# Graph and mixture-of-experts layers on one core: groups of two tiles in the second pass, and an expert's second products two steps behind its first

## The chip, the cores and the metric

The kernel runs on one core of a Trainium2 chip. The metric is the device time of one execution in microseconds (us): 2432.77 us, the median of three runs from 2429.38 to 2436.04. The profiled execution took 2431.52 us with a span of 2429.8 us; 1.7 us lie outside the span.

## The reference, cut to what matters

3125 nodes of 256 numbers pass two layers. Each layer adds a sum over a graph (103,125 edges) and an attention, then a mixture of eight experts. The change touches the second layer alone:

```
xn = layernorm(x)
agg = segment_sum((xn @ W[type])[src, type], dst)          # gathered rows, summed by target node
h = gelu(agg + xn @ loop_w + h_bias + xn)
x = x + layernorm(h) * ln_gamma + ln_beta + attention(xn)
xn = layernorm(x) * gamma + beta
w = softmax over the two largest of xn @ Wr + br           # 0 for the six other experts
for e in range(8):
    y = y + w[e] * (gelu(xn @ W1[e] + b1[e]) @ W2[e] + b2[e])   # W1 256x512, W2 512x256
x = x + y
```

All eight experts are computed for every node, in 32-bit floats.

## The kernel before, in words

The nodes are sorted by their number of edges and stand in 25 tiles of 128; tile 24 has 53 of them. `x` stays in SBUF for the whole kernel. The first layer writes a table of rows to HBM (`htab_f`); the second layer is the "second pass" of this text.

**Gathers.** The row sum of tile t takes STEPS[t] gathers (45 for tile 0 down to 22 for tile 24). Each is an indirect DMA that GpSimd (POOL) issues, and fetches one row of 256 numbers for each of the 128 nodes (L195). `edge_pass` (L1336) does the tiles in the order of GROUPS1 (L69). It takes up to four gathers at a time into a buffer `gt` (a *chunk*, L1358), and adds the chunk up on VectorE (DVE) with L1376 and a last addition L1378. The pool of `gt` has five buffers (L2013), so the gathers of a chunk can't start before the chunk five before it has been added. The tiles 1 to 4 (PAIRS) are gathered before that, in `first_groups` (L2572, additions in L2590).

**Groups.** When all tiles of a group are summed, its jobs go into a list (`after1`, L2544, `Group`, L2312). First come ten jobs that lead to the routing: `sums_a` to `sums_c` (the products with `loop_w`, L2326 to L2328, added by L2333, and a Gelu), `states_a` to `states_d` (two layer norms, with square roots on ScalarE (ACT), L2353), `routes_a` (transposes L2396 and the routing products L2404, both in a PSUM tile `pt`), `routes_b` (the two largest, L206 to L223 and L2417) and `shares` (the constants of the experts, L2456 and L2481). Then come ten steps (`step`, L2492). Step i takes what the step before left in PSUM (`take`, L2489 on DVE), issues the first products of expert i (`hidden`, L2436 on TensorE (PE), with a Gelu on ACT, L2441, into a buffer `hT1`), and the second products of expert i-1 (`outputs`, L2470) into one of two PSUM banks (`bank`, L2445). The last four steps of a group are put between the first jobs of the next group (`late`, L2542). Below, h3 stands for the `hidden` of expert 3, o3 for its `outputs`, and "loops" for the products L2326 to L2328.

**The order of the work.** After each chunk, `edge_pass` runs jobs worth a credit (L1383 to L1391): what the list costs divided by the gathers left in the group, kept between 0.9 and 1.3, for each gather. A job's cost is the number beside it in `jobs` (L2502). The order on DVE and POOL is exactly this program order (`manual_schedule`, L2601); PE's, ACT's and SP's order is the scheduler's. So a `take` stands on DVE between the additions of two chunks, and whatever it waits for, the next chunk's additions wait for too. The results of all tiles leave at the end, by scatters on POOL (L242).

Before the change the groups are, in order: tiles (3,4), (1,2), (23,24), (19 to 22), (15 to 18), (12 to 14), (9 to 11), (7,8), 6, 5 and 0.

Of the kernel before, what the change touches and what calls it, by code (L numbers as in the profile page):

```python
# [12 lines left out]
F32 = mybir.dt.float32  # L13
# [8 lines left out]
P = 128  # L22
# [11 lines left out]
NX = 8  # L34
F = 512
FC = F // P
# [27 lines left out]

MADE = tuple(range(1, 25)) + (0,)

CUTS1 = (25, 23, 19, 15, 12, 9, 7, 6, 5)
PAIRS = ((3, 4), (1, 2))
GROUPS1 = tuple(range(a, b + 1) for a, b in PAIRS) + tuple(range(b, a) for a, b in zip(CUTS1, CUTS1[1:])) + (range(0, 1),)  # L69

# [32 lines left out]
def gps_kernel(ctx: ExitStack, tc: tile.TileContext, a, out):  # L103
# [1216 lines left out]
    def fast():  # L1320
# [197 lines left out]
        def hidden(ts):  # L1518
            n, at0 = len(ts) * P, ts[0] * P
            for i in range(2):  # L1520
                if i not in hTs:
                    hTs[i] = f0h.tile([P, FC, 3 * P], F32, name=f"hT0_{i}", bufs=1)
                hT = hTs[i]
                for f in range(FC):
                    ph = ps_mm.tile([P, 512], F32, name="mm")
                    for c in range(2):
                        PE.matmul(  # L1527
                            ph[:, :n], w1[:, i, c, f * P : (f + 1) * P], xT[:, c, at0 : at0 + n],
                            start=(c == 0), stop=(c == 1),
                        )  # L1530
                    S.activation(hT[:, f, :n], ph[:, :n], AF.Gelu, bias=b1[:, i, f : f + 1])
# [57 lines left out]
        with ExitStack() as l0x:  # L1589
# [257 lines left out]
            class Fin0:  # L1847
# [46 lines left out]
                def jobs(self):  # L1894
                    def step(i):
                        if i < self.k:
                            self.products(i)
                        if i > 0:
                            self.sums(i - 1)

                    out = [(5.0 if 0 < i < self.k else 2.5, lambda i=i: step(i)) for i in range(self.k + 1)]
                    return out + [(2.0 * self.k, self.norms)]
# [21 lines left out]
            def after0(g, tiles, accs):  # L1924
                last = g == len(GROUPS) - 1
                if last:
                    fin[0].accs = accs
                    return
                bg.extend(Fin0(tiles, accs).jobs())
                if g == SURE:  # L1930
                    bg.extend(staged(guess(), (4.0, 3.0, 3.0, 2.0, 2.0, 2.0)))
                    for r in range(NX):
                        bg.extend(staged(relation(r), (1.5, 1.5)))
                for ts in GROUPS[: g + 1] if g == SURE else [tiles] if g > SURE else []:
                    bg.append((5.0 * len(ts), lambda ts=ts: hidden(ts)))
                    if waiting:
                        bg.append(waiting.pop())
                    bg.append((4.0 * len(ts), lambda ts=ts: (outputs_a(ts), outputs_out(ts))))
                    waiting.append((1.0 * len(ts), lambda ts=ts: outputs_b(ts)))
                if g == len(GROUPS) - 2:  # L1940
                    bg.append((4.0, lambda: None))
                    bg.append(waiting.pop())
                if g == len(GROUPS) - 2:
                    fin.append(Fin0(GROUPS[-1], None))
                    bg.append((2.5, lambda: fin[0].products(0)))
# [34 lines left out]
        with tc.If(again > 0):  # L1980
            w_full, rank = settled
            pick = f0k.tile([P, 2, NX], F32, name="pick")
            for i in range(2):
                V.tensor_scalar(pick[:, i, :], rank[:, 0, :], float(i), None, op0=ALU.is_equal)
            load_pair(pick)
            tmp = f0k.tile([P, NX], F32, name="tmp_c")
            V.tensor_tensor(tmp, w_full[:, 0, :], pick[:, 0, :], op=ALU.mult)
            V.reduce_sum(w_first, tmp, axis=AX.X)
            for ts in GROUPS:
                k = len(ts)  # L1990
                mv = small.tile([P, 4, 2], F32, name="mv1")
                rs = small.tile([P, 4], F32, name="rs1")
                for j, t in enumerate(ts):
                    V.tensor_tensor(x[:, t, :], x[:, t, :], bet, op=ALU.subtract)
                    stats(x[:, t, :], mv[:, j, :])
                rstd(mv[:, :k, :], rs[:, :k])
                for j, t in enumerate(ts):
                    normalize(xt_tok[:, t, :], x[:, t, :], mv[:, j, :], rs[:, j : j + 1])
                    V.tensor_tensor(x[:, t, :], x[:, t, :], bet, op=ALU.add)
                    to_xT(t, xt_tok[:, t, :])  # L2000
                if ts == GROUPS[-1]:
                    for i in range(2):
                        hidden_gelus(i, hidden_products(ts, i, phs[i]))
                else:
                    hidden(ts)
                    outputs_a(ts)
                    outputs_out(ts)
                    outputs_b(ts)
# [176 lines left out]
        with ExitStack() as l1x:  # L2185
# [20 lines left out]
            wf = l1w.tile([P, NT, NX], F32, name="wf")  # L2206

            fin = l1x.enter_context(tc.tile_pool(name="fin1", bufs=1))
            f1 = l1x.enter_context(tc.tile_pool(name="f1", bufs=3))
            wp = l1x.enter_context(tc.tile_pool(name="wp", bufs=1))  # L2210
            w1s, w2s = [None] * NX, [None] * NX

# [99 lines left out]
            class Group:  # L2312
# [114 lines left out]

                def hidden(self, e):
                    n, at0 = self.n, self.at0
                    hT = self.hT[e] = f1.tile([P, FC, 4 * P], F32, name="hT1")  # L2430
                    fs, w = max(4 // self.k, 1), self.k * P
                    for f0 in range(0, FC, fs):
                        ph = ps_mm.tile([P, 512], F32, name="mm")
                        for f in range(f0, min(f0 + fs, FC)):
                            for c in range(2):
                                PE.matmul(  # L2436
                                    ph[:, (f - f0) * w : (f - f0) * w + n], w1s[e][:, c, f * P : (f + 1) * P],
                                    xT[:, c, at0 : at0 + n], start=(c == 0), stop=(c == 1),
                                )
                        for f in range(f0, min(f0 + fs, FC)):  # L2440
                            S.activation(  # L2441
                                hT[:, f, :n], ph[:, (f - f0) * w : (f - f0) * w + n], AF.Gelu, bias=b1[:, e, f : f + 1]
                            )
# [48 lines left out]
                def step(self, i):  # L2492

                    self.take()
                    if i < NX:
                        self.hidden(i)
                    if 1 <= i <= NX:
                        self.outputs(i - 1)
                    if i == NX + 1:
                        leaving.extend(self.tiles)  # L2500

                def jobs(self):  # L2502
                    k = self.k
                    first = [
                        (2.0, self.sums_a), (2.0, self.sums_b), (1.0, self.sums_c), (1.0, self.states_a),
                        (1.0, self.states_b), (1.0, self.states_c), (1.0, self.states_d), (4.0, self.routes_a),
                        (2.0, self.routes_b), (2.0, self.shares),
                    ]
                    cost = [1.6] + [3.1] * (NX - 1) + [1.6, 0.5]
                    rest = [(c * k, lambda i=i: self.step(i)) for i, c in enumerate(cost)]  # L2510
                    return first, rest

# [100 lines left out]
    with tc.If(unfit < 1):  # L2613
        fast()
# [78 lines left out]
```

## Time and profile before

| what | us |
|---|---|
| median of three runs | 2432.77 |
| profiled execution | 2431.52 |
| its span | 2429.8 |
| second pass: its first gather ends | 1493 |
| last gather of the second pass starts | 2344.28 |
| last gelu jobs (tile 0, L2333) start | 2377.86 |
| last `take` starts | 2420.36 |
| last scatter starts | 2421.12 |

The page gives for each engine its busy time in the span, in 40 slices, and by groups of instructions. POOL's part in the second pass is an almost unbroken line of gathers: each is shown as busy for about 0.95 us, with 0.30 us of issue before it. The timeline gives every instruction with its start, its length, and in brackets how long its engine sat idle before it and for what. Adjoining instructions of one kind are merged into one row (x16). "PEclk" is the clock that PE was granted, as a share of full speed.

### The profile page before, as it was taken

Reading aid. Unit: us, or ns where it says so; the run is one execution under the profiler, and the core shown is the slowest. Engines: PE = TensorE matmul, PEld = TensorE weight load, DVE = VectorE, ACT = ScalarE, POOL = GpSimd, SP = SyncE. Lnnn points to the kernel's source line nnn. Section 1 sums busy time; section 2 is a strip of 40 time slices with the busy share of each in tenths; the row PEclk is TensorE's granted clock in tenths of the full one; section 3 lists DMA queues with packets and bytes.
Section 4 is the critical chain, followed back from the end, with each engine's and each line's share of the span. In section 5 each row is a group of like instructions: output and inputs, shape, how many; then the busy total and the mean of one; then the engine's idle time right before and its main releaser. Section 6 shows DMA issues by size and latency. Waiting matters only on the chain.

```text
span 2429.8 us, 20895 instructions
## 1 busy us (share of the span) xinstructions
PE 1689.2 (70%) x6033; PEld 1106.3 (46%) x6033; DVE 1236.6 (51%) x3393; ACT 532.4 (22%) x1263; POOL 1705.9 (70%) x1847
## 2 busy tenths in 40 slices
PE   3446697502946526267699836988687899989997
PEld 2323344301624313145344324766354566667786
DVE  7655555525534434344567435554543636465542
ACT  4313231001201101012222222322211222132343
POOL 4577777777777777777126777677777777777771
PEclk9777887855978667687799977998798999999999
DMA  6544434344444344444156754333333333333330
GB/s 197 146 109 110 110 105 129 105 108 137 108 107 107 105 109 106 108 105 107 58 186 240 268 166 149 94 104 103 108 101 110 104 104 110 107 103 103 102 101 19
DMA packets 124809, 289.03 MB, mean 119 GB/s; under 512 B 41258, under 2 KB 62830, under 8 KB 121480
## 3 DMA queue, kind: packets, MB, share of 16 engines
q0 software_dynamic: 83184, 230.02, 34.3%
q1 hardware_dynamic: 36970, 54.83, 6.7%
q10 hardware_dynamic: 4526, 2.71, 0.4%
q8 instruction: 51, 0.84, 0.1%
q14 instruction: 78, 0.64, 0.1%
HBM read 248.54 MB, written 38.89 MB: 118 GB/s over the span
## 4 chain that ended last, share of the span: by engine, by line
PE 23%; POOL 9%; issue 8%; DVE 5%; DMA 4%; ACT 1%; DVEq 0%; POOLq 0%; ACTq 0%
POOL gt L195 8%; PE mm L2436 7%; PE py L2470 7%; PE mm L190 7%; DMA gt<-htab_f,idx2g 3%; DVE gt L1376 1%; POOL out_dram L242 1%; DVE bnst L164 1%; PE pt L2404 1%; PE mm L2328 1%; PE mm L2326 0%; DVE x L2369 0%; DVE acc L1378 0%; DVE x L2489 0%; DVE hh L2368 0%
## 5 line engine op out<-in xcount | busy, mean ns | idle before, releaser
L195 POOL DMA_INDIRECT gt<-btab,idx x764 | 742.9, 972 | 232.7 <-issue 193.4
L195 POOL DMA_INDIRECT gt<-htab_f,idx2g x718 | 704.2, 981 | 225.0 <-issue 192.5
L1369 DVE TENSOR_TENSOR run<-run,gt 128x512 f32<-128x512 f32 (+1 forms) x400 | 266.9, 667 | 470.7 <-DMA gt<-btab,idx 468.9
L2470 PE MATMUL py<-w,hT 128*128 128x256 f32 (+1 forms) x1600 | 376.8, 391 | 46.4 <-DVE x L2489 46.4
L2436 PE MATMUL mm<-xT,w 128*128 128x256 f32 (+4 forms) x1408 | 377.1, 422 | 5.9 <-DVE x L2334 5.9
L2470 PEld LDWEIGHTS py<-w,hT 128*128 128x128 f32 (+1 forms) x1600 | 305.4, 194 | 111.8 <-DVE x L2489 26.4
L2436 PEld LDWEIGHTS mm<-xT,w 128*128 128x128 f32 x1408 | 249.4, 203 | 109.3 <-issue 68.1
L1376 DVE TENSOR_TENSOR gt<-gt 128x512 f32<-128x512 f32 (+1 forms) x344 | 182.6, 531 | 175.3 <-DMA gt<-htab_f,idx2g 168.9
L2441 ACT ACTIVATE hT<-mm,b 128x256 f32<-128x256 f32 (+4 forms) x352 | 158.5, 493 | 393.9 <-PE mm L2436 393.7
L190 PE MATMUL pt<-w_own,xT 128*128 128x256 f32 x100 | 38.8, 524 | 265.9 <-DVE acc L1869 265.9
L190 PE MATMUL mm<-w_rel,xT 128*128 128x512 f32 x400 | 175.0, 595 | 3.5 <-ACT xT L185 3.5
L2489 DVE SCALAR_TENSOR_TENSOR x<-py,wf,x 128x256 f32<-128x256 f32 x200 | 87.1, 477 | 143.8 <-PE py L2470 143.8
L190 PEld LDWEIGHTS pt<-w_own,xT 128*128 128x128 f32 x100 | 23.8, 261 | 277.2 <-DVE acc L1869 270.9
L195 POOL DMA_INDIRECT gt<-htab_f,soon x96 | 93.5, 974 | 53.3 <-issue 20.1
L190 PEld LDWEIGHTS mm<-w_rel,xT 128*128 128x128 f32 x400 | 74.9, 190 | 95.8 <-issue 84.2
L1527 PE MATMUL mm<-xT,w 128*128 128x384 f32 (+2 forms) x320 | 96.8, 468 | 16.2 <-DMA w<-in_f_W_dram 16.2
L190 PE MATMUL mm<-w_qkv,xT 128*128 128x512 f32 (+1 forms) x200 | 90.5, 564 | 19.0 <-ACT vs L1775 18.5
L1876 ACT ACTIVATE rs<-rs 128x3 f32<-128x3 f32 (+2 forms) x11 | 2.2, 203 | 446.1 <-DVE rs L1875 446.1
L1556 PE MATMUL mm<-w,hT 128*128 128x256 f32 x400 | 97.5, 399 | 0.0
L1887 PE MATMUL pmean<-ones,xt 128*128 128x1 f32 (+1 forms) x100 | 21.2, 315 | 105.8 <-DVE xt L173 105.8
L1556 PEld LDWEIGHTS mm<-w,hT 128*128 128x128 f32 x400 | 77.1, 198 | 30.8 <-issue 20.5
L1527 PEld LDWEIGHTS mm<-xT,w 128*128 128x128 f32 x320 | 64.2, 221 | 48.3 <-DMA w<-in_f_W_dram 14.9
(441 smaller groups left out, 2214.7 us busy)
## 6 DMA issues: line engine op xcount, KB each, us to landing
htab_f<-hs SPq DMA_DIRECT2D x25, 1024.0 KB
gt<-btab,idx POOLq DMA_INDIRECT x764, 2.8
gt<-htab_f,idx2g POOLq DMA_INDIRECT x718, 2.8
w<-in_f_W_dram SPq DMA_DIRECT2D x20, 512.0 KB
ntab<-x SPq DMA_DIRECT2D x5, 640.0 KB
btab<-bs SPq DMA_DIRECT2D x5, 640.0 KB
x<-in_x_dram SPq DMA_DIRECT2D x4, 640.0 KB
otab<-xn SPq DMA_DIRECT2D x12, 128.0 KB
```

Of the source, the lines that this page charges most:

```text
L164: V.bn_stats(out=st, in_=src)
L190: PE.matmul(ps, lhs[:, c, t * P : (t + 1) * P], w[:, c, :], start=start and c == 0, stop=stop and c == 1)
L195: G.indirect_dma_start(out=dst, out_offset=None, in_=table, in_offset=bass.IndirectOffsetOnAxis(ap=idx, axis=0))
L242: G.indirect_dma_start(out=table, out_offset=bass.IndirectOffsetOnAxis(ap=idx, axis=0), in_=src, in_offset=None)
L1369: V.tensor_tensor(d, d, gt[:, k1 - b : k1 - a, :], op=op)
L1376: V.tensor_tensor(gt[:, :h, :], gt[:, :h, :], gt[:, m - h : m, :], op=op)
L1527: PE.matmul(ph[:, :n], w1[:, i, c, f * P : (f + 1) * P], xT[:, c, at0 : at0 + n], start=(c == 0), stop=(c == 1),)
L1556: PE.matmul(py[:, i * D : (i + 1) * D], hTs[i][:, f, j * P : (j + 1) * P], w2[:, i, f, :], start=False, stop=(f == FC - 1), skip_group_che ...
L2436: PE.matmul(ph[:, (f - f0) * w : (f - f0) * w + n], w1s[e][:, c, f * P : (f + 1) * P], xT[:, c, at0 : at0 + n], start=(c == 0), stop=(c == 1),
L2441: S.activation(hT[:, f, :n], ph[:, (f - f0) * w : (f - f0) * w + n], AF.Gelu, bias=b1[:, e, f : f + 1])
L2470: PE.matmul(py[:r, j * D : (j + 1) * D], hT[:, f, at : at + r], w2s[e][:, f, :], start=(f == 0), stop=(f == FC - 1),)
L2489: V.scalar_tensor_tensor(d, y, wf[:r, t, e : e + 1], d, op0=ALU.mult, op1=ALU.add)
```

## The change

The groups of three and four tiles become pairs, and the tiles' order changes with them; each step's `outputs` belong to the expert two steps back; a group has eleven steps instead of ten, so the four late ones are now h7 with o5, o6, o7 and the end (before: h6 with o5, h7 with o6, o7 and the end). The buffers `hT1` hold two tiles instead of four, and there are four instead of three.

```
-CUTS1 = (25, 23, 19, 15, 12, 9, 7, 6, 5)
+CUTS1 = (25, 23, 21, 19, 17, 15, 13, 11, 9, 7, 6, 5)
...
-            f1 = l1x.enter_context(tc.tile_pool(name="f1", bufs=3))
+            f1 = l1x.enter_context(tc.tile_pool(name="f1", bufs=4))
...
-                    hT = self.hT[e] = f1.tile([P, FC, 4 * P], F32, name="hT1")
+                    hT = self.hT[e] = f1.tile([P, FC, 2 * P], F32, name="hT1")
...
                     self.take()
                     if i < NX:
                         self.hidden(i)
-                    if 1 <= i <= NX:
-                        self.outputs(i - 1)
-                    if i == NX + 1:
+                    if 2 <= i <= NX + 1:
+                        self.outputs(i - 2)
+                    if i == NX + 2:
                         leaving.extend(self.tiles)
...
-                    cost = [1.6] + [3.1] * (NX - 1) + [1.6, 0.5]
+                    cost = [1.6, 1.6] + [3.1] * (NX - 2) + [1.6, 1.6, 0.5]
```

After the change the groups are: (3,4), (1,2), (23,24), (21,22), (19,20), (17,18), (15,16), (13,14), (11,12), (9,10), (7,8), 6, 5 and 0: fourteen instead of eleven.

## The prediction

> **What bounds the kernel now.** I read the 40 slices first, then the groups and the waits of the second pass, then the timelines of PE, POOL and DVE.
>
> ```profile
> PE   3446697502946526267699836988687899989997
> ...
> POOL 4577777777777777777126777677777777777771
> ```
>
> POOL is equally busy in every slice of the second pass (slices 25 to 39); 7 is as full as it gets, since each gather has 0.30 us of issue before it that doesn't count as busy. PE swings from 5 to 9. The groups and waits between 1480 us and the end say the same:
>
> ```profile
> L195 POOL DMA_INDIRECT gt<-htab_f,idx2g x662 | 647.7, 978 | 208.0 <-issue 178.2 <-DVE acc L1378 12.7 <-DVE gt L1376 5.2
> ```
> ```profile
> DVE x L2489 <- PE py L2470: 143.8, 53, 6.7
> ...
> PEld py L2470 <- ACT hT L2441: 0.9, 3, 0.3
> ```
>
> A gather takes 0.978 + 0.30 = 1.28 us, and 653 of them fill the time from 1493 to 2345 us. DVE waits 143.8 us for PE's second products, and that costs POOL almost nothing, as five buffers (20 gathers, some 25 us) lie between. POOL does stand still when DVE is later than that. In the whole pass this happens three times, at 1539, 1551 and 1575 us (1.02 - 0.30 = 0.7, 3.4 and 2.2 us: 6.3 us together). Two of them:
>
> ```profile
> 1551.52 1.15 POOL L195 DMA_INDIRECT gt<-htab_f,idx2g  x1 [3.72 <-DVE acc L1378]
> ...
> 1575.62 0.94 POOL L195 DMA_INDIRECT gt<-htab_f,idx2g  x1 [2.50 <-DVE acc L1378]
> ```
>
> So the end is POOL's line up to the last gather, and then a tail. Its landmarks in the timeline:
>
> ```profile
> 2344.28 1.13 POOL L195 DMA_INDIRECT gt<-htab_f,idx2g  x1 [0.30 <-issue]
> ...
> 2377.86 0.42 DVE L2333 TENSOR_TENSOR acc<-acc,mm 128x256 f32<-128x256 f32 x1 [5.57 <-PE mm L2328]
> ...
> 2421.12 0.96 POOL L242 DMA_INDIRECT out_dram<-x,id_i  x1 [32.85 <-DVE x L2489]
> ```
>
> In the tail PE works off tile 5's experts, then tile 0's, 3.51 us each. **Two things can move the time: when POOL's line ends, and how long the tail is.**
>
> **What one pair of tiles needs on PE now.** At 1490 to 1620 us the groups (3,4) and (1,2) run one behind the other, with DVE late and all data there, so PE's own order sets the pace:
>
> ```profile
> 1543.18 1.02 PE L2326 MATMUL mm<-w_lu,xT 128*128 128x512 f32 x2
> ...
> 1548.26 3.62 PE L2436 MATMUL mm<-xT,w 128*128 128x256 f32 x16
> 1551.71 7.07 PE L2470 MATMUL py<-w,hT 128*128 128x256 f32 x32
> 1562.38 1.23 PE L2396 MATMUL pt<-ident,hh 128*128 128x128 f32 x4 [3.60 <-DVE hh L173]
> ...
> 1566.42 8.22 PE L2436 MATMUL mm<-xT,w 128*128 128x256 f32 x26
> ```
> ```profile
> 1561.00:1562.00 1.00, 0.00 (x0) 0.50 0.47 131
> 1562.00:1563.00 1.00, 0.62 (x3) 0.50 0.42 131
> 1570.00:1571.00 1.00, 1.00 (x4) 0.50 0.46 131
> 1571.00:1572.00 1.00, 1.00 (x6) 0.89 0.43 131
> ```
>
> Loops 5.1 us (1543.18 to 1548.26), then h7, o6, o7 at 3.45 each, 3.6 us idle until the states have gone through DVE and ACT, transposes at 1562.38. The third column of the second view is the clock: after the idle it is 0.50 until 1571. The first o0 ends at 1580.3, 17.9 us after the transposes; the next loops start at 1615.58. One cycle: 72.4 us.
>
> **The change, part by part.**
>
> *Second products two steps behind.* The wait this could remove, of second products for a Gelu, is 0.9 us in the whole pass (second of the waits above). What it does move is work: in the built program's order PE now has h7 o5, loops, o6, o7 and then the transposes, so only two blocks instead of three lie beside the states. The transposes come 19.2 us after the loops' start now (1562.38 - 1543.18) with three chunks added on DVE in between; two of the new groups keep three, the others have two (an addition of a chunk is 1.6 us): 19.2 or 17.6. PE's own work is done after 5.1 + 6.9 = 12.0, so it idles 5.6 to 7.2 us instead of 3.6. After the transposes h2 stands before o0: 17.9 + 3.45 = 21.4, then five blocks of h and o, 34.5. Sum: 73.5 or 75.1; I take **74 us a pair cycle**, between 69 (were the idle and half the cold stretch filled) and 78 (were each of them longer by half).
>
> *Pairs instead of fours.* PE's products cost by their columns: 16 of 512 columns take 6.87 us, of 256 3.45, of 128 1.78 (chain of work), so 384 more first products, each narrower, cost nothing. ACT gets 64 Gelus of 0.467 us for four tiles instead of 32 of 0.687, 8 us more on an engine busy for 220 of 865 us; PE's 6.9 us an expert hide the 1.9 us that a pair's Gelus take, and without that cover they would be added eight times a cycle. The `hT1` buffers cost nothing (one is spare either way), nor does SP's swap of two weight loads: `w_lu`, issued at 1386 us, comes forward, and PE first reads it at 1463. But a pair's states, routing and cold restart come once for two tiles instead of once for four, and the order fixes how many gathers go by in a cycle. Counted in the built program's order on DVE from one group's gelu jobs to the next, at 1.28 us a gather and 1.31 for an `own_i` row:
>
> | from, to | gathers | POOL's time | short of 74 |
> |---|---|---|---|
> | (1,2), (23,24) | 51 + 3 own | 69.2 | 4.8 |
> | (23,24), (21,22) | 53 + 2 own | 70.5 | 3.5 |
> | (21,22), (19,20) | 53 + 1 own | 69.2 | 4.8 |
> | (19,20), (17,18) | 51 | 65.3 | 8.7 |
> | (17,18), (15,16) | 54 | 69.1 | 4.9 |
> | (15,16), (13,14) | 58 | 74.2 | 0 |
> | (13,14), (11,12) | 65 | 83.2 | 0 |
>
> Before, the cycle after (1,2)'s gelus had 61 gathers (78 us), and the fours gave PE slack: DVE's lateness, 27.5 us at gather 42 (its gathers end at 1547.8, the chunk's addition at 1575.3), was down to 4 at gather 77. Now DVE stays at the limit of the five buffers, and POOL waits what a cycle is short. Queued behind each late `take` on DVE are the next chunks' additions; POOL waits for those, and nothing gives its time back. Sum 26.7 us; the stalls of 6.3 us that are there now become 3.4 longer, since (3,4)'s first o0 has h2 before it. **POOL's line ends 30 us later.**
>
> *The tail.* At the last chunk 15 takes are left instead of 17, and tile 5's routing stands before it instead of behind it. Tile 5's gelu job stands behind gather 630, now summed at 2319 us; the cycle from (7,8) to 6 is 53 gathers, 67.8 us, so 6 us short of 74: 2325. To its transposes 10.6 us (2337.3 to 2347.9 now), then to tile 0's gelu 30.0 (2347.9 to 2377.9) plus 1.8 for h7 ahead of the loops: 2367.4, 10.4 earlier. Behind it ACT's table load for the square root no longer waits for h7's Gelus: DVE had its sum at 2379.93 and the root came at 2382.16, 2 us. From there on nothing changes, 3.51 us an expert on PE. **The tail is 12 us shorter.**
>
> **Sum**, against the profiled execution (2431.5; the median of the runs shown is 1.3 more): 2431.5 + 30 - 12 = **2450 us**.
>
> [...] Here 3.6 us of idle did cost the clock, and it came back after 8.7 us (1562.38 to 1571). [...]
>
> **Rivals.**
>
> *PE keeps up; faster (the other side).* In a cycle of at most 69 us POOL is short in one cycle only. For it: PE's bare work in a cycle is 72.4 - 3.6 idle - about 4 cold = 65 us, it idles 92 of the 852 us between 1493 and 2345, and pairs hand it work sooner. Against it: the two cycles that the trace shows both took 72. It decides from 69 us down. Then 3.4 us are lost at the start, and the tail gains 12 + 5: 2431.5 + 3.4 - 17 = 2418.
>
> *As costly as now.* A cycle of 72: short by 2.8, 1.5, 2.8, 6.7, 2.9, sum 16.7; tail 14: 2431.5 + 20.1 - 14 = 2438, within what can't be told from no change.
>
> *Each gap longer.* A cycle of 78, because DVE, late, comes to the states later than PE's order allows: short by 50.5, tail 8: 2431.5 + 53.9 - 8 = 2477.
>
> **How the numbers follow.** Forecast 0.45; PE keeps up 0.2; as costly as now 0.2; longer 0.15. About 0.3% (7 us) is what a measurement of this kernel can tell from no change. Faster by more: 0.2. Within: 0.17, most of "as costly as now". Slower: 0.63. The range reaches from 2417 (PE keeps up) to 2476 (almost all of "longer").
>
> **What would show it.** Right: POOL rows with several us of "DVE acc L1378" between 1580 and 1900 us, together some 36 us in the pass; the last gather starting near 2374; loops 73 to 76 us apart for the pairs up to (15,16), with PE at 0.50 for 8 us after each group's transposes; tile 0's L2333 some 23 us behind the last gather's start instead of 33.6. Wrong: a last gather within 5 us of 2344 (then PE keeps up), loops 69 us apart or less, or stalls of POOL that something else releases.

## The result, and the profile after

The changed kernel takes 2445.6 us (median of five runs, 2443.34 to 2447.55), the kernel before 2432.77 beside it (five runs): the ratio is 1.0058, with a 95% interval of 1.0047 to 1.007. It is **slower by 13 us** by the medians (14 by the ratio). The forecast was 2450. A second comparison on another chip (the last experiment) gives 1.0038, 1.0026 to 1.0051, which is 9 us.

The profiled execution took 2445.6 us with a span of 2443.9. The slices, POOL's gathers between 1490 and 2376 us, and one of the waits between 1480 us and the end:

```profile
PE   3446697502936516166799847989998889878987
...
POOL 5577777777777777777036777677767777777772
```
```profile
L195 POOL DMA_INDIRECT gt<-htab_f,idx2g x656 | 641.4, 978 | 232.3 <-issue 172.1 <-DVE acc L1378 38.4 <-DVE rsh L2380 5.9
```
```profile
DVE x L2489 <- PE py L2470: 197.1, 60, 5.2
```

A gather lasts 978 ns as before, and POOL's line is still the frame of the pass. What has grown is the idle time that DVE's additions (L1378) release, from 12.7 to 38.4 us, and DVE's waits for second products, from 143.8 to 197.1 us. Two of POOL's stalls, from its timeline:

```profile
1577.82 0.94 POOL L195 DMA_INDIRECT gt<-htab_f,idx2g  x1 [5.23 <-DVE acc L1378]
...
1799.42 0.94 POOL L195 DMA_INDIRECT gt<-htab_f,idx2g  x1 [3.84 <-DVE acc L1378]
```

There are sixteen, from 1536 to 1945 us, where before there were three, all before 1576 us. Summed, each less the usual 0.30 us of issue, they are 32.3 us instead of 6.3. The landmarks of the tail, from the timelines of POOL and DVE:

```profile
2372.32 0.95 POOL L195 DMA_INDIRECT gt<-htab_f,idx2g  x1 [0.30 <-issue]
...
2393.32 0.42 DVE L2333 TENSOR_TENSOR acc<-acc,mm 128x256 f32<-128x256 f32 x1 [5.57 <-PE mm L2328]
...
2434.78 0.96 POOL L242 DMA_INDIRECT out_dram<-x,id_i  x1 [29.91 <-DVE x L2489]
```

The last gather starts 28.0 us later (2344.28 before; 2.2 of it come from the first pass, as the second pass's first gather ends 2.2 us later), but tile 0's L2333 follows it after 21.0 us instead of 33.6. So the line is longer and the tail shorter, and the line wins.

The first pass varies from run to run: the second pass's first gather ends anywhere from 1491.5 to 1500.2 us in the profiles below. So I compare the profiled kernels from that gather on. "Line" is from its end to the last gather's end, "tail" from there to the span's end, "stalls" is POOL's idle time above 0.30 us within the line. Each is one execution, as the profile took it; the ratios are of medians.

| kernel | line | stalls in it | tail | pass | ratio to before |
|---|---|---|---|---|---|
| before: fours, one step behind | 852.3 | 6.3 | 84.4 | 936.7 | 1 |
| after: pairs, two steps | 877.9 | 32.3 | 70.6 | 948.6 | 1.0058 [1.0047, 1.007] |
| pairs, one step | 864.9 | 17.2 | 71.9 | 936.8 | 1.0000 [0.999, 1.001] |
| fours, two steps | 860.0 | 11.8 | 92.5 | 952.5 | 1.0062 [1.0047, 1.0077] |
| after, seven gather buffers | 868.6 | 22.7 | 69.9 | 938.5 | 1.0011 [1.0002, 1.002] |
| after, PE kept busy before the transposes | 867.5 | 16.4 | 69.1 | 936.6 | 0.9995 [0.9986, 1.0005] |
| after, on another chip | 876.3 | 29.5 | 70.6 | 947.0 | 1.0038 [1.0026, 1.0051] |

Line less stalls is 845.6 to 848.2 us in all but one (851.1): the gathers don't change, only the waiting does. The four experiments in the middle ran on one chip, where the kernel before took 2437.15 us. The changed kernel itself was not run on that chip, so what an experiment gains on it is a difference of two ratios, and I give it against both of its comparisons (1.0058 and 1.0038).

### The profile page after: what moved, and what is told of

It reads as the page before. It is cut to its first block, busy times and chain, and to the rows that moved or that the text cites. A ratio compares the mean times of both kernels' runs of the same rounds, so it can differ in the third digit from the quotient of the medians.

```text
span 2443.9 us, 21868 instructions
## 1 busy us (share of the span) xinstructions
PE 1705.4 (70%) x6417; PEld 1190.8 (49%) x6417; DVE 1247.9 (51%) x3467; ACT 563.5 (23%) x1391; POOL 1709.4 (70%) x1847
## 4 chain that ended last, share of the span: by engine, by line
PE 31%; DVE 7%; issue 5%; POOL 5%; DMA 3%; ACT 1%; DVEq 0%; POOLq 0%; ACTq 0%
PE mm L2436 13%; PE py L2470 9%; PE mm L190 6%; POOL gt L195 5%; DMA gt<-htab_f,idx2g 2%; DVE gt L1376 1%; DMA gt<-htab_f,soon 1%; PE pt L2404 1%; PE mm L2328 1%; DVE bnst L164 1%; PE mm L2326 1%; DVE x L2489 1%; DVE acc L1378 0%; PE py L2456 0%; PE mm L2327 0%
## 5 line engine op out<-in xcount | busy, mean ns | idle before, releaser
L2436 PE MATMUL mm<-xT,w 128*128 128x256 f32 (+2 forms) x1792 | 400.9, 380 | 0.0
L2470 PE MATMUL py<-w,hT 128*128 128x256 f32 (+1 forms) x1600 | 367.6, 383 | 14.6 <-DVE x L2489 14.6
L2436 PEld LDWEIGHTS mm<-xT,w 128*128 128x128 f32 x1792 | 334.3, 208 | 45.3 <-issue 7.1
L2470 PEld LDWEIGHTS py<-w,hT 128*128 128x128 f32 (+1 forms) x1600 | 299.9, 189 | 68.6 <-issue 24.8
L2441 ACT ACTIVATE hT<-mm,b 128x256 f32<-128x256 f32 (+2 forms) x448 | 170.9, 440 | 346.7 <-PE mm L2436 346.4
L2489 DVE SCALAR_TENSOR_TENSOR x<-py,wf,x 128x256 f32<-128x256 f32 x200 | 88.3, 478 | 197.1 <-PE py L2470 197.1
L190 PEld LDWEIGHTS mm<-w_rel,xT 128*128 128x128 f32 x400 | 74.9, 190 | 95.8 <-issue 84.2
L190 PE MATMUL mm<-w_qkv,xT 128*128 128x512 f32 (+1 forms) x200 | 91.8, 572 | 18.9 <-ACT vs L1775 18.4
L1527 PEld LDWEIGHTS mm<-xT,w 128*128 128x128 f32 x320 | 61.7, 212 | 46.8 <-DMA w<-in_f_W_dram 15.1
```

What stands on the lines that cost most here:

```text
L190: PE.matmul(ps, lhs[:, c, t * P : (t + 1) * P], w[:, c, :], start=start and c == 0, stop=stop and c == 1)
L1527: PE.matmul(ph[:, :n], w1[:, i, c, f * P : (f + 1) * P], xT[:, c, at0 : at0 + n], start=(c == 0), stop=(c == 1),)
L2436: PE.matmul(ph[:, (f - f0) * w : (f - f0) * w + n], w1s[e][:, c, f * P : (f + 1) * P], xT[:, c, at0 : at0 + n], start=(c == 0), stop=(c == 1),
L2441: S.activation(hT[:, f, :n], ph[:, (f - f0) * w : (f - f0) * w + n], AF.Gelu, bias=b1[:, e, f : f + 1])
L2470: PE.matmul(py[:r, j * D : (j + 1) * D], hT[:, f, at : at + r], w2s[e][:, f, :], start=(f == 0), stop=(f == FC - 1),)
L2489: V.scalar_tensor_tensor(d, y, wf[:r, t, e : e + 1], d, op0=ALU.mult, op1=ALU.add)
```

## The experiments

The theory is that of the prediction: a pair's cycle on PE, with its idle time and half clock before the transposes, is a little longer than the gathers that the order puts beside it; DVE stays at the limit of the five buffers, and POOL pays the difference. The rivals: the pairs cost it and the distance of two steps doesn't (or the other way round); POOL's stalls cost nothing, as the tail sets the end.

**Pairs, one step behind.** The changed kernel with the second half of the change undone:

```
-                    if 2 <= i <= NX + 1:
-                        self.outputs(i - 2)
-                    if i == NX + 2:
+                    if 1 <= i <= NX:
+                        self.outputs(i - 1)
+                    if i == NX + 1:
...
```

> The changed kernel's pairs, with an expert's second products one step behind its first, as before. Theory (the pairs cost POOL's line, the second step of distance adds a little): a pair cycle of 72 us instead of 74, h2 no longer ahead of the first o0, so the stalls of POOL in the second pass fall from 32 us to about 19; the tail stays short, some 5 us longer than with the distance of two. Time about 2437 us. Rival (the distance of two is what costs): stalls back to the 6 us of the kernel before and a short tail, about 2420 us.

Measured: 2437.67 us, ratio 1.0000 [0.999, 1.001]. The pairs alone are worth nothing: their line is 12.6 us longer and their tail 12.5 us shorter. So the loss comes with the second step. The tail is 1.3 us longer than with two steps (71.9 and 70.6), where 5 were expected. PE's timeline shows where the second step costs. Here is one cycle with one step behind, from the products of the loops (L2326) to the transposes (L2396):

```profile
1823.60 1.02 PE L2326 MATMUL mm<-w_lu,xT 128*128 128x512 f32 x2
...
1828.67 3.62 PE L2436 MATMUL mm<-xT,w 128*128 128x256 f32 x16
1832.13 7.07 PE L2470 MATMUL py<-w,hT 128*128 128x256 f32 x32
1842.78 1.22 PE L2396 MATMUL pt<-ident,hh 128*128 128x128 f32 x4 [3.58 <-DVE hh L173]
```

and the same group in the changed kernel:

```profile
1838.37 1.02 PE L2326 MATMUL mm<-w_lu,xT 128*128 128x512 f32 x2
...
1843.45 7.10 PE L2470 MATMUL py<-w,hT 128*128 128x256 f32 x32
1856.61 1.22 PE L2396 MATMUL pt<-ident,hh 128*128 128x128 f32 x4 [6.06 <-DVE hh L173]
```

The block h7 (the 16 products of L2436) is gone from beside the states; it was done before the loops. PE has 3.45 us less to do there and idles 2.5 us more. From these loops to the next: 71.7 us with one step, 74.0 with two. The six cycles from the loops of (1,2) to those of (13,14) are 1.2 to 3.2 us longer each with two steps, 13 us together; the stalls differ by 15 (17.2 and 32.3). In these six cycles PE is busy 401.6 us with two steps and 401.8 with one, and it waits for no `take` (L2489). The states don't come later either: from the loops to the transposes it is 18.4 us on average with two steps and 19.4 with one. What differs is how long PE idles before the transposes (two steps, then one step: us in the six cycles, times, longest):

```profile
PE pt L2396 <- DVE hh L173: 36.8, 6, 7.3
...
PE pt L2396 <- DVE hh L173: 23.4, 6, 5.2
```

That is 13.4 us, and the cycles together are 13.4 us longer. So in the pairs the missing work beside the states accounts for the whole difference.

**Fours, two steps behind.** The kernel before with the other half of the change, the same lines the other way round.

> The groups of the kernel before (up to four tiles), with an expert's second products two steps behind. Theory: the fours still give PE slack after tile 24, so POOL stands still for 6 to 12 us, and the tail is that of the kernel before less about 2 us (the square root's table load no longer waits for h7's Gelus). Time about 2434 us. Rival (the distance of two is what costs): POOL's line 20 us or more later, 2450 us.

Measured: 2452.63 us, ratio 1.0062 [1.0047, 1.0077]. The theory's 2434 us is missed by 18.6 us as it stands, and by some 13 to 14 if the slower time of the kernel before on that chip is allowed for. The rival's time (2450) fits, its reason only in part: the line is not 20 us later. What the theory missed is in two places: the line is 7.7 us longer (5.5 of it stalls; the prediction had 3.4 at the start), and the tail 8.1 us longer, where it expected nothing. PE's timeline of the group of tiles 7 and 8 shows the second. Before the change (one step):

```profile
2225.74 5.32 PE L2436 MATMUL mm<-xT,w 128*128 128x384 f32 x16
2230.90 5.34 PE L2470 MATMUL py<-w,hT 128*128 128x256 f32 x24
2237.89 5.42 PE L2470 MATMUL py<-w,hT 128*128 128x256 f32 x24 [1.65 <-DVE x L2489]
2243.14 0.60 PE L2396 MATMUL pt<-ident,hh 128*128 128x128 f32 x4
```

and with two steps:

```profile
2240.76 5.45 PE L2470 MATMUL py<-w,hT 128*128 128x256 f32 x24 [1.63 <-DVE x L2489]
2250.58 8.42 PE L2470 MATMUL py<-w,hT 128*128 128x256 f32 x24 [4.37 <-DVE x L2489]
2258.84 0.60 PE L2396 MATMUL pt<-ident,hh 128*128 128x128 f32 x4
```

o6 and o7 each need a bank that a `take` on DVE must empty first, and DVE is at the states. With h7 between them and the loops, PE waits 1.65 us; without it 1.63 + 4.37, and o7 then begins at half clock (PEclk is 0.50 at 2251 us, 1.00 at 2257 and 0.63 on average from 2250 to 2259) and takes 8.42 us instead of 5.42 for the same products. The loops of tiles (7,8), 6, 5 and 0 come 77.2, 44.0 and 41.5 us apart instead of 71.3, 42.7 and 40.5: 8.2 us, which is the tail. So two steps behind costs 9 to 14 us with pairs (the two comparisons of the changed kernel) and 15 with fours; with pairs it is all stalls, with fours half of it is tail. The theory of the line was right for the pairs, but incomplete: PE's backlog behind the last gather can be lengthened in the same way.

**Seven gather buffers.** The changed kernel, with two more buffers `gt`, in a pool of their own that takes two of every seven chunks:

```
+            gp2 = l1x.enter_context(tc.tile_pool(name="gp2", bufs=2))
...
-                    gp, h_rows, D, lambda t: idx2[:, t, :], ALU.add, bg, lambda g, *a: after1(g + 2, *a),
+                    Seven(), h_rows, D, lambda t: idx2[:, t, :], ALU.add, bg, lambda g, *a: after1(g + 2, *a),
```

> The changed kernel with seven gather buffers in edge_pass instead of five. Theory (POOL waits for a buffer because DVE stands behind PE): DVE may be later by two more chunks, eight gathers, 10 us, once; the stalls fall from 32 us to about 22 and the time by the same, to about 2435 us; the pair cycles on PE stay at 74 us. Rival (POOL's line is later for another reason, the gathers themselves or HBM): no change, 2445 us.

Measured: 2438.81 us, ratio 1.0011 [1.0002, 1.002], 0.47% or 11 us less than the changed kernel by the first ratio, 0.27% or 7 us by the second. Stalls 22.7 us instead of 32.3, line 9.3 us shorter. PE's work is the same, so POOL's stalls do set the end, and they come from DVE's lateness against the buffers. It is a loan, though: two buffers let DVE be later once by two chunks' gathers, and the cycles are still short of gathers.

**PE kept busy before the transposes.** The changed kernel with twelve products that nobody reads (the profile shows 24 rows, two for each), ahead of each group's last normalisation:

```
                 def states_d(self):
...
+                    pw = ps_tr.tile([P, 512], F32, name="pt")
+                    for i in range(12):
+                        PE.matmul(pw[:, :D], ident, w1s[0][:, 0, :D], start=True, stop=True)
```

> The changed kernel with 12 products that nobody reads (256 columns, 5.2 us at full clock) on PE after o7, in the idle time before the next group's transposes, so that PE's clock stays full. Nothing else changes. Theory (a cold restart costs each pair some 4 us): PEclk stays near 1.00 behind the transposes, a pair cycle is 70 us instead of 74, the stalls of POOL fall from 32 to about 12 us, and the tail loses two cold restarts, some 6 us. Time about 2420 us, though PE does more. Rival (the clock is not what makes the cycle long, the Gelus' and routing's latency is): 2445 us or up to 20 us more, as the extra work delays the transposes.

Measured: 2436.6 us, ratio 0.9995 [0.9986, 1.0005]: adding 5.34 us of useless work to each group on PE takes back the whole loss. PE's timeline:

```profile
1777.53 5.34 PE L2388 MATMUL pt<-w,ident 128*128 128x256 f32 x24
1783.46 0.76 PE L2399 MATMUL pt<-ident,hh 128*128 128x128 f32 x4 [0.58 <-DVE hh L173]
```

and two of its stretches of 1 us (busy times of PE, PEld, DVE, ACT, POOL, then PEclk):

```profile
1783.00:1784.00 1.00, 0.54 (x4) 0.41 (x4) 1.00 (x3) 0.00 (x0) 0.83 (x1) 1.00 0.37 111
1784.00:1785.00 1.00, 0.45 (x4) 0.24 (x3) 0.96 (x4) 0.85 (x2) 0.69 (x2) 1.00 0.16 49
```

The clock stays at 1.00 behind this group. In the changed kernel, with its idle of 6.06 us before the transposes at 1856.61:

```profile
1858.00:1859.00 1.00, 0.94 (x3) 0.93 (x4) 1.00 (x4) 0.46 (x2) 0.61 (x1) 0.50 0.45 127
...
1864.00:1865.00 1.00, 1.00 (x3) 0.78 (x3) 0.00 (x0) 0.99 (x2) 0.70 (x2) 0.50 0.46 131
1865.00:1866.00 1.00, 1.00 (x6) 0.85 (x5) 0.00 (x0) 0.98 (x2) 0.89 (x1) 0.93 0.47 131
```

It is 0.50 until 1865, 8.5 us after the transposes began. The cycles that were 74.9, 74.0, 72.9, 74.0 and 75.2 us are 72.2, 70.8, 70.2, 70.6 and 72.0 (that of tiles 23 and 24 stays at 69.3), 15 us together, and the stalls fall from 32.3 to 16.4. The gain in time, 0.63% or 15 us by the first ratio and 0.43% or 10 us by the second, is less than the 25 expected. Keeping the clock is worth 2.7 to 3.4 us in those five cycles and nothing in the sixth: behind tiles 23 and 24 PE is at 0.50 again from 1646 us, with no gap longer than 1.57 us around it, and the mean clock of that cycle is 0.95 (it is 0.98 in the first and 1.00 in the four others). The tail is 1.5 us shorter where 6 were expected. And the gathers of that run took 986 ns instead of 978, 5 us in 653; why they did, no run shows.

**More of PE's own work beside the states.** If h7 is what is missing, it can be put back without undoing the two steps, by letting the four late steps stand one place later among the next group's first jobs, behind the loops:

```
-                    if late and i in (0, 3, 5, 7):
+                    if late and i in (3, 5, 7, 8):
```

This was run with the changed kernel (three times), with pairs and one step (twice) and with the kernel before; and the unread products (seven of them) with pairs and one step. **These runs can't answer the question.** They fell on chips where the kernel before itself takes 2985 to 2991 us, 23% more than on the others.

> The changed kernel (pairs, two steps behind) with one line different: the four late steps stand one place later in the next group's first jobs, so h7 with o5 comes behind the loops' products instead of before them. TensorE then has four blocks (h7, o5, o6, o7) beside the layer norms of the states instead of two (o6, o7). Theory A (two steps behind cost time because only o6 and o7, which wait for takes, are left beside the states, so that PE idles 5 to 9 us and restarts at half clock): the idle before a pair's transposes falls from 5.5-8 us to under 1.5, the clock stays at 1.00 through them, a pair's cycle falls from 74 to 66-68 us, POOL's stalls in the pass from 32 to 8-14 us, and the ratio to the kernel before is 0.992 to 0.997. Rival B (the distance of two steps costs time by itself, through the takes that stand between a chunk's additions, wherever the late steps stand): the cycles stay at 72-75, stalls at 25-35 us, ratio 1.004 to 1.007.

> Pairs, one step behind, with the same one-line shift of the late steps: h6, o5, h7, o6, o7 stand beside the states instead of h7, o6, o7. Theory A (what counts is PE work beside the states): the idle before the transposes goes from 3.6 us to nothing and the clock stays at 1.00, cycles of 65-68 us, the same as with two steps behind and the same shift: ratio 0.992 to 0.997, within 0.2% of that kernel. Rival B (the distance by itself): this one is faster than the two-steps kernel with the shift by 0.4% or more, some 10 us.

> Pairs, one step behind, and at the beginning of each group's last normalisation seven products of 256 columns that nobody reads (3.1 us of PE), so that PE isn't idle for 3.6 us before the transposes. The late steps are not shifted. Theory (the restart at half clock is some 3 us of each pair's 72.4 us, as the dummies in the two-steps kernel took 2.5 to 3.6 us from each cycle): cycles of 69-70 us, POOL's stalls from 17 to 5-10 us, the tail behind the last gather some 3 us shorter, ratio 0.994 to 0.997. Rival (the clock costs nothing here, as DVE's states and routing set the cycle): cycles of 72, ratio 1.000.

> The kernel before (groups of up to four, one step behind) with only the one-line shift of the late steps. Theory: the fours have idle time of PE before the transposes only in their first groups and slack for it, so POOL's line gains little (stalls 6 to 2-6 us); the tail behind the last gather, with single tiles, loses its idle and restarts, 84 to 74-80 us: ratio 0.995 to 0.998. Rival (the tail is PE's work that is left over at the last gather and has no slack to give): ratio 0.999 to 1.002.

> The same kernel as e9_late_beside_lag2, again, because on the chip of that run the kernel before, too, took 23% longer (2988 us, with PE waiting several us at a time for nothing that the trace shows), so POOL's gathers were not what bounded it. Theory A (two steps behind cost time because only o6 and o7 stand beside the states): where the kernel before takes its usual 2430 to 2440 us, no idle before a pair's transposes (below 1.5 us), clock 1.00 through them, pair cycles of 66-68 us instead of 74, POOL's stalls 8-14 us instead of 32, ratio 0.992 to 0.997. Rival B (the distance of two steps costs by itself, through the takes between the additions): cycles 72-75, stalls 25-35 us, ratio 1.004 to 1.007.

> The same kernel as e10_late_beside_lag1, again, for the same reason. Theory A (what counts is PE work beside the states): no idle before the transposes, cycles of 65-68 us, ratio 0.992 to 0.997 and within 0.2% of the two-steps kernel with the same shift. Rival B (the distance by itself): this one is faster than the two-steps kernel with the shift by 0.4% or more, some 10 us.

> The kernel of e9_late_beside_lag2 a third time, for the case that the kernel before takes its usual 2430 to 2440 us beside it. Theory A (two steps behind cost time because only o6 and o7, which wait for takes, stand beside the states): no idle before a pair's transposes (below 1.5 us), clock 1.00 through them, pair cycles of 66-68 us instead of 74, POOL's stalls 8-14 us instead of 32, ratio 0.992 to 0.997. Rival B (the distance of two steps costs by itself): cycles 72-75, stalls 25-35 us, ratio 1.004 to 1.007. Where the kernel before takes over 2900 us again: ratio 1.008 to 1.016 as in the two runs before, and nothing more can be read from it.

| kernel | us | before beside it | ratio |
|---|---|---|---|
| pairs, two steps, late steps shifted | 3013.91 | 2988.25 | 1.0121 [1.0081, 1.016] |
| the same, again | 3013.4 | 2985.02 | 1.0114 [1.0061, 1.0167] |
| the same, third | 3025.08 | 2990.63 | 1.0100 [1.0062, 1.0138] |
| pairs, one step, late steps shifted | 2991.11 | 2988.25 | 0.9985 [0.9948, 1.0021] |
| the same, again | 2982.87 | 2985.02 | 1.0015 [0.9978, 1.0051] |
| pairs, one step, unread products | 2995.37 | 2988.25 | 1.0034 [1.0002, 1.0066] |
| kernel before, late steps shifted | 3005.3 | 2988.25 | 1.0057 [1.002, 1.0095] |

PE's timeline of the first of them shows why they say little of the other chips:

```profile
2173.89 1.03 PE L2436 MATMUL mm<-xT,w 128*128 128x256 f32 x4
2175.48 0.46 PE L2436 MATMUL mm<-xT,w 128*128 128x256 f32 x1 [0.56 <-issue]
2176.18 0.38 PE L2436 MATMUL mm<-xT,w 128*128 128x256 f32 x1 [0.24 <-issue]
2177.59 0.38 PE L2436 MATMUL mm<-xT,w 128*128 128x256 f32 x1 [1.03 <-issue]
2178.32 0.76 PE L2436 MATMUL mm<-xT,w 128*128 128x256 f32 x1 [0.35 <-issue]
2181.11 1.31 PE L2436 MATMUL mm<-xT,w 128*128 128x256 f32 x2 [2.03 <-issue]
```

In the middle of a block whose data are all there, PE stands still for up to 2 us between two products, waiting for nothing that the profile shows. A gather takes 974 ns there and 978 in the changed kernel, but POOL's stalls in the pass are 280 us and the pairs' cycles 86 to 112 us, so POOL's gathers no longer set the pace. Nor is it PE alone: between 1763 us and the end ACT waits 286.0 us before its Gelus (L2441) and DVE 253.8 us before its takes (L2489) for something that the profile can't name. Two things can still be read. Of the thirteen groups after the first, eleven have no idle before the transposes, the other two 0.48 and 0.26 us: the shift does fill that place. And on these chips the distance isn't free even so: with the same shift, two steps are slower by 1.4 and 1.0% than one step by the ratios, in both cases that the two ran side by side. That speaks there for the rival of these runs, that the distance costs by itself, and I can't say what in the trace makes it. Besides, the shift has a price of its own with one step: Gelus of h6 and h7 then fall between the states' square roots, and ACT reloads its tables 37 times for L2353 and 49 for L2441 (1.28 us each), instead of 14 and 27 in the shifted kernel with two steps.

Whether the shift would make the pairs faster than the kernel before where that takes 2437 us stays open.

**The changed kernel, again,** meant as the base for those runs:

> [...] Theory A (PE work beside the states is what two steps behind takes away): the unshifted kernel is slower than the shifted one (1.0100 to 1.0121 to the kernel before), by half a per cent or more: ratio 1.015 to 1.025, with several us of idle before the transposes, which the shifted kernel doesn't have. [...] Should the kernel before take its usual 2430 to 2440 us: ratio 1.0045 to 1.007 as in the first comparison.

It fell on a chip of the usual time: 2445.5 us beside 2435.98, ratio 1.0038 [1.0026, 1.0051], a little under the 1.0045 to 1.007 expected for that case. Stalls 29.5 us, tail 70.6: the profile after, once more. It gives no base for the runs above. No kernel here is faster than the kernel before beyond its interval.

## Why the prediction was right, step by step

*The end is POOL's line, then a tail.* Right: line less stalls is 845.9 us before and 845.6 after, and two more buffers alone, which leave the pairs' cycles on PE as they were, give 7 to 11 us back.

*A pair cycle of 74 us.* Right: 74.9, 74.0, 72.9, 74.0 and 75.2 us in the cycles up to (13,14), with 5.5 to 7.3 us of idle before the transposes (5.6 to 7.2 foretold). One is off: 69.3 us from (23,24) to (21,22). Tile 24 has 53 nodes instead of 128, which I had in the table of `own` rows but not in PE's columns.

*POOL waits what a cycle is short.* The sum was right, the split less so. Foretold: 9.7 us at the start and then 4.8, 3.5, 4.8, 8.7, 4.9, 0, together 36.4. Found: 12.9 for the first two together, then 2.1 (the cycle of tile 24), 1.7, 8.3, 3.4 and 3.9, together 32.3. The longest stretch without slack, (19,20) to (17,18), has the largest stall, as the table of gathers said. POOL's last gather started 28.0 us later for 30 foretold, but 2.2 of the 28.0 are the first pass's, which the prediction left out: the line itself is 25.6 us longer. So the line was foretold 4.4 us too long, and the first pass, by chance, made up for half of it in the time.

*The tail is 12 us shorter.* Right: 84.4 to 70.6, so 13.8. One term on the way was off: from the loops of (7,8) to those of tile 6 it is 79.5 us, not 74. Tile 0's L2333 still came 21.0 us behind the last gather's start, 23 foretold; what made up for the term no run separates, so this number is in part luck.

*The clock.* The step took 8.7 us at 0.50 from one row; in the nine groups of the changed kernel from (1,2) to (9,10) the clock came back 6.9 to 10.1 us after the transposes began. In a group of one tile it came back sooner: in the kernel before, tile 6's transposes begin at 2307.5 us and the clock is 1.00 again at 2311.9, 4.4 us later. That the half clock is part of the cost is shown by the unread products, not only argued.

*Where the gain went.* The wait that two steps behind could remove was 0.9 us, as said. What the prediction didn't part is the two halves: its sum for a cycle as costly as now (2438, which is 6 us more than before: a line 20 longer and a tail 14 shorter) comes near what pairs with one step give (2437.67 with the kernel before at 2437.15, which is 0.5 more: line 12.6 longer, tail 12.5 shorter). So the pairs with one step were no loss, and the second step is the whole of it.

*Missed altogether:* that two steps behind also lengthens the tail where groups are large. The forecast needed it nowhere, as in the pairs the tail is no longer than with one step (70.6 and 71.9), but the expectation for the fours with two steps failed by it.

## What to carry to other kernels

A deeper distance between two halves of a pipeline moves work from behind a point to before it. Before doing it, list for the longest chain of small steps on the other engines which blocks stand beside it on the busy engine, and which of these need nothing from that chain; here one such block (h7, 3.45 us in each cycle) was worth 9 to 14 us of 2433. Where one engine is a line that never recovers lost time, count its work between two fixed points of the order, cycle by cycle: an average (PE busy 70%) hides that one cycle of 73 us had only 65 us of gathers beside it.

## What the runs showed of the hardware

In the nine groups of the changed kernel from (1,2) to (9,10) PE idled 5.5 to 9.1 us before the transposes. In each its clock fell to 0.50 in that time, 2.1 to 5.3 us after the last product, and came back 6.9 to 10.1 us after the transposes began. These stretches at 0.50 lasted 10.2 us in five of the groups and 13.7 us in the other four. A dozen products that nobody reads kept the clock at 1.00 in four of the six cycles compared, and were worth 0.4 to 0.6% of the kernel.

The kernel before takes 2433 to 2437 us on some chips and 2985 to 2991 us on two others. It was profiled only on the usual ones; the shifted kernel on a slower chip, held against the changed kernel on a usual one, shows single products and gathers of the same length (a gather 974 and 978 ns, sixteen products of 256 columns 3.62 us on both), but engines that stand still within their own streams: PE 76.7 us before L2436, and none in the changed kernel. What the engines wait for there the profile doesn't show.
